# Reading the ids into registers before batch 10 instead of along the way

## The chip, the cores and the metric

The kernel runs on one core of a Trainium2 chip. The metric is the device time of one execution in microseconds (us); lower is better. A core has five engines with a program each: TensorE (PE), VectorE (DVE), ScalarE (ACT), GpSimd (POOL) and SyncE (SP). In front of each engine stands a sequencer, which takes the engine's instructions in their order, keeps registers, and hands work on to the engine.

## The reference

128 batches of a 128 x 512 f32 tile each go through an adapter whose weights are picked by an id of the batch (0 to 9), then a layer norm with gamma and beta of that id, then a residual:

```
w1, w2 = W1[ids], W2[ids]                          # (B,512,128), (B,128,512)
h = relu(einsum('bsh,bha->bsa', x, w1) + b1[ids])
y = x + einsum('bsa,bah->bsh', h, w2) + b2[ids]
n = (y - mean(y)) * rsqrt(var(y) + 1e-5)
out = x + n * gamma[ids] + beta[ids]
```

## The kernel before

W2 and the ten rows of beta, gamma and b2 (spread over all partitions) stay in SBUF for the whole run. Each batch passes through these steps, named in the code: `transpose_x` (PE, L490) and `copy_xT` (ACT, L494) turn x; `down` (PE, L513) multiplies by W1; `relu` (ACT, L521) adds b1; `up` (PE, L535) multiplies by W2 into a PSUM tile `py`, of which there are five; `residual` (DVE, L553) adds x and b2 and sums the rows, after `vector_b2` (DVE, L545) in some batches; `square` (ACT, L576) sums the squares; for a pair of batches `scalar_means` (ACT, L567), `deviation` (ACT, L586) and three small steps `rstd` (DVE, L590, L592, L595) make mean and deviation; `scale` (DVE, L619) multiplies by gamma; `finish` (DVE, L628) adds x plus beta, which `add_beta` (POOL, L507) has made in the tile `o`; `store` (SP, L632) writes a pair of batches. `add_b2` (POOL, L500) makes x plus b2 in one of four tiles `r` for about two thirds of the batches. W1 of a batch comes by a transfer that SP issues or by a copy from SBUF (`stage_w1`, ACT L481, or POOL).

Each of these steps that uses a row of a table needs the batch's id in a register of its own engine. The ids lie in SBUF in two forms: `lang`, one word a batch, and `packed`, 27 words of four ids each for batches 20 to 127 (`NEAR` is 20, `FAR` is 27). A read is a `TENSOR_LOAD` (L271), an instruction of the engine's sequencer. `near` reads four words of `lang` (batches 0-3, 4-7 and so on), `far` four words of `packed` (three at the end), each once an engine; what has been read is kept. So ACT, PE and DVE make five reads of `lang` and seven of `packed` each. `far_at_once` reads all 27 words on POOL. SP reads for its transfers when it comes to them.

The order of instructions on each engine is the order in which the Python code calls the steps (`keep` pins it). The first calls are written out by hand. Then each step is put on a list with a due time in batches (`at`), mostly from the tables `STEPS`, and the list is sorted by due time; the last batches are again written out by hand. So a read whose due time changes moves among the same other steps of its engine, which keep their order.

Of the kernel before, what the change touches and what calls it, by code (L numbers as in the profile page):

```python
# [13 lines left out]
ET = mybir.EngineType  # L14
# [3 lines left out]
G = 4  # L18
# [125 lines left out]
def cond_resid_kernel(ctx: ExitStack, tc: tile.TileContext, x, itok, W1, b1, W2, b2, gamma, beta, out):  # L144
# [18 lines left out]
    def keep(ins):  # L163

        engine = ins.ins.engine
        if engine in last:
            tc.add_manual_dep(ins.ins, last[engine], behind, reason="kept order")
        last[engine] = ins.ins.name
        return ins
# [21 lines left out]
    def xb(b):  # L191
        return xs[b // X][:, b % X, :]
# [62 lines left out]
    NEAR, BITS = 20, 5  # L255
    FAR = (B - NEAR) // 4
# [13 lines left out]
    def read_ids(tile, engine, most, why):  # L270
        loads, vals = nc.values_load_multi_w_load_instructions(  # L271
            tile, engines=[engine], min_val=0, max_val=most, skip_runtime_bounds_check_because=why
        )
        for ins in loads:
            keep(ins)
        return vals

    def near(b, engine):
        g = b // G
        if (g, engine) not in lids:  # L280
            lids[g, engine] = read_ids(
                lang[0:1, g * G : (g + 1) * G], engine, L - 1, "clamped on the chip to 0..L-1 above"
            )
        return lids[g, engine][b % G]
# [13 lines left out]
    def far_at_once(engine):  # L298
        vals = read_ids(packed, engine, ((1 << 4 * BITS) - 1) * H, "four ids of 0..L-1 at five bits each, times H")
        for i in range(0, FAR, G):  # L300
            lids[(NEAR + i) // G, engine] = vals[i : i + G]
# [8 lines left out]
    def lid_h(b, engine):  # L310

        if b < NEAR:
            return near(b, engine) * H
        k, v = far(b, engine)
        if k:
            v = v >> (BITS * k)
        v = v & (((1 << BITS) - 1) * H)
        return v.with_bounds(min_val=0, max_val=(L - 1) * H, guaranteed_mod_val=0, out_of_modulus=H)
# [67 lines left out]
    def spread(r, copier):  # L386
        t = (beta_b, gamma_b, b2_b)[r // L]
        row = p_y.tile([P, H], FP, tag="y", name=f"row_{r}")
        pick_r = pick[:, r : r + 1].to_broadcast([96, P])
        keep(nc.tensor.matmul(row, lhsT=pick_r, rhs=parts[:96, :], start=True, stop=True))  # L390
        dst = t[:, r % L * H : (r % L + 1) * H]
        if copier is nc.scalar:
            keep(nc.scalar.copy(dst, row))
        else:
            keep(nc.vector.tensor_copy(dst, row))
# [21 lines left out]
    def of(parts, b):  # L417
        if b < len(parts[0]):
            return parts[0][b]
        return parts[1][b % steady] if b < closing else parts[2][b - closing]  # L420
# [4 lines left out]
    def turn(b):  # L425
        return of(TURNS, b)
# [4 lines left out]
    def seeded(b):  # L431
        return kind(b) in SEEDED

    def b2_on_gpsimd(b):
        return kind(b) in ON_GPSIMD

    def b2_by_vector(b):
        return kind(b) == "D"
# [63 lines left out]
    def add_beta(b):  # L502
        g, j = divmod(b, 2)
        if g not in os:
            os[g] = op.tile([P, 2, H], FP, tag="o", name=f"o_{g}")
        v = lid_h(b, ET.Pool)
        keep(nc.gpsimd.tensor_tensor(os[g][:, j, :], xb(b), beta_b[:, bass.ds(v, H)], ALU.add))  # L507
# [283 lines left out]
    spread(18, nc.scalar)  # L791
    spread(19, nc.scalar)
    far_at_once(ET.Pool)
    add_beta(0)
    add_beta(1)
    spread(20, nc.scalar)
# [13 lines left out]
    def at(when, step, *args):  # L810
        plan.append((when, len(plan), step, args))

    def when(name, b):
        return b + of(STEPS[name], b)

    for b in range(B):
        if b >= 20 and b % X == 0:
            at(b + X_STEPS[b // X - 10], load_x, b // X)
        if b >= 3:
            for n, engine in ((b + 5, ET.Activation), (b + 5, ET.PE), (b + 6, ET.Pool)):  # L820
                if n < NEAR:
                    at(b + 0.99, lid, n, engine)
        if turn(b) in "Fw":
            at(when("load", b), load_rows if turn(b) == "F" else load_late, b)
        if turn(b) == "F":
            at(when("load", b), load_blocks, b)
            at(when("turn", b), turn_blocks, b)
        elif 5 <= b <= E - 2:
            at(when("transpose", b), transpose_x, b)
            at(when("copy", b), copy_xT, b)  # L830
        if 4 <= b <= E - 3:
            if b2_on_gpsimd(b):
                at(when("r", b), add_b2, b)
            at(when("beta", b), add_beta, b)
            at(when("down", b), down, b)
            at(when("relu", b), relu, b)
        if seeded(b):
            at(when("seed", b), seed, b)
        if FIRST <= b <= E - 1 and turn(b) not in "Fw":
            at(when("w1", b), stage_w1, b)  # L840
        if 2 <= b <= E - 4:
            at(when("up", b), up, b)
# [4 lines left out]
    def at_pair(g, key, step, *args):  # L847
        if g < E // 2 - 3 or (step, *args) in begun:
            at(key, step, *args)

    for g in range(E // 2 - 1):
        b = 2 * g
        for n in (b, b + 1):
            if b2_by_vector(n):
                at_pair(g, when("vb2", n), vector_b2, n)
            at_pair(g, when("stat", n), residual, n)
            at_pair(g, when("square", n), square, n)
        at_pair(g, when("means", b), scalar_means, g)
        at_pair(g, when("root", b), deviation, g)
        for n in (1, 2, 3):  # L860
            at_pair(g, when(f"n{n}", b), rstd, g, n)
        for n in (b, b + 1):
            at_pair(g, when("scale", n), scale, n)
            at_pair(g, when("end", n), finish, n)
        if b % G == 0 and b + G < NEAR:
            at_pair(g, when("scale", b) + 0.001, lid, b + G, ET.DVE)
        at_pair(g, when("store", b), store, g)

    for n in range(0, FAR, G):
        for engine, first in ((ET.Activation, 6.5), (ET.PE, 6.3), (ET.DVE, 7.0)):  # L870
            at(first + n / 2, far, NEAR + n, engine)

    for _, _, step, args in sorted(plan, key=lambda step: step[:2]):
        step(*args)
# [185 lines left out]
```

## Time and profile before

| | |
|---|---|
| time, median of 3 runs (lowest, highest) | 301.47 us (300.65, 301.47) |
| the profiled execution | 300.83 us |
| its span, first to last instruction | 299.1 us |
| busy of the span: PE, DVE, ACT, POOL | 290.8, 288.9, 273.4, 276.3 us |
| granted clock of TensorE | 0.996 |

The profiled execution is a run of its own, 0.64 us below the median; 1.73 us of it lie outside the span. A sequencer's instructions, the reads among them, are not counted as busy; they show as rows of the queues PEldq, ACTq, DVEq, POOLq and SPq. In the rows of groups and lines the numbers of buffers are left out.

### The profile page before, as it was taken

The numbers are of one execution on the slowest core, as the hardware profiler recorded it, in microseconds if no ns is written. First come the engines' busy times: TensorE is split into PE (matmuls) and PEld (weight loads), VectorE is DVE, ScalarE is ACT, GpSimd is POOL, SyncE is SP. The second block draws the span as 40 slices with busy tenths as digits, with TensorE's granted clock in tenths as the row PEclk, the third lists the DMA queues.
The fourth block names the chain that finished last, engine by engine and source line by source line (L and its number), as shares of the span: only waits on it lengthen the run. The fifth ranks groups of instructions, "written<-read, shape, count | busy, mean of one in ns | idle before, by whom it ended". The sixth has DMA issues, their size and how long they took to land. (4 is left out here: it accounts for less than half of the span.)

```text
span 299.1 us, 8487 instructions
## 1 busy us (share of the span) xinstructions
PE 290.8 (97%) x1779; PEld 216.3 (72%) x1779; DVE 288.9 (97%) x780; ACT 273.4 (91%) x760; POOL 276.3 (92%) x238
## 2 busy tenths in 40 slices
PE   7999998999999999999999999999999999999992
PEld 3868776777777777777777777777777777777760
DVE  6999998999999999999999999999999999999995
ACT  4877886999999999999999999999999999899992
POOL 1199998998999999999999999999999999999982
PEclk9999999999999999999999999999999999999998
DMA  6999999989487997869995997859976898993816
GB/s 228 384 388 369 343 312 407 360 287 286 168 279 245 312 390 229 317 206 345 323 301 179 276 403 249 323 191 328 346 226 253 277 355 265 307 346 121 272 50 234
DMA packets 62260, 85.82 MB, mean 287 GB/s; under 512 B 4185, under 2 KB 26212, under 8 KB 62210
## 3 DMA queue, kind: packets, MB, share of 16 engines
q1 hardware_dynamic: 62150, 85.23, 83.8%
q8 instruction: 16, 0.26, 0.4%
q14 instruction: 34, 0.28, 0.3%
q10 hardware_dynamic: 60, 0.05, 0.1%
HBM read 51.71 MB, written 33.55 MB: 285 GB/s over the span
## 5 line engine op out<-in xcount | busy, mean ns | idle before, releaser
L507 POOL TENSOR_TENSOR o<-x,beta_b 128x512 f32<-128x512 f32 x121 | 153.6, 1304 | 12.6 <-DVE beta_b L408 12.6
L513 PEld LDWEIGHTS ph<-xT,w1s 128*128 128x128 f32 x1024 | 126.9, 192 | 15.1 <-ACT hT L521 9.1
L513 PE MATMUL ph<-xT,w1s 128*128 128x128 f32 x1024 | 135.7, 275 | 1.2 <-ACT sq L576 1.1
L500 POOL TENSOR_TENSOR r<-x,b_b 128x512 f32<-128x512 f32 x83 | 106.7, 1305 | 2.9 <-DVE part L592 2.2
L535 PE MATMUL py<-w,hT 128*128 x196 | 100.5, 595 | 0.0
L490 PEld LDWEIGHTS pxT<-ident,x 128*128 128x128 f32 x464 | 60.2, 151 | 52.5 <-issue 38.0
L619 DVE SCALAR_TENSOR_TENSOR py<-py,nmean,gamma_b 128x512 f32<-128x512 f32 x124 | 92.5, 751 | 0.3
L576 ACT ACTIVATE sq<-py,sum 128x512 f32<-128x512 f32 x124 | 86.1, 694 | 2.8 <-DVE py L553 1.0
L628 DVE SCALAR_TENSOR_TENSOR o<-py,rstd,o 128x512 f32<-128x512 f32 x116 | 84.9, 746 | 2.7 <-issue 1.5
L494 ACT COPY xT<-pxT 128x512 f32<-128x512 f32 x116 | 68.3, 588 | 7.9 <-PE pxT L490 6.5
L490 PE MATMUL pxT<-ident,x 128*128 128x128 f32 x464 | 71.3, 277 | 0.1
L553 DVE SCALAR_TENSOR_TENSOR py<-py,r 128x512 f32<-128x512 f32 x88 | 60.7, 690 | 0.0
L521 ACT ACTIVATE hT<-ph,b1T 128x128 f32<-128x128 f32 x128 | 47.7, 373 | 4.8 <-PE ph L513 2.4
L481 ACT COPY w1s<-w 128x512 f32 x80 | 48.7, 622 | 0.2
L535 PEld LDWEIGHTS py<-w,hT 128*128 128x128 f32 x196 | 30.1, 192 | 1.8 <-issue 1.1
L527 PE MATMUL py<-w,hT 128*128 x60 | 30.8, 595 | 0.0
L576 ACT ACTIVATION_READ_ACCUMULATOR sq<-py,sum 128x1 f32 x124 | 25.9, 209 | 0.0
L553 DVE SCALAR_TENSOR_TENSOR py<-py,b_b 128x512 f32<-128x512 f32 x30 | 20.6, 687 | 0.0
L473 ACT COPY py<-x 128x512 f32<-128x512 f32 x30 | 18.0, 599 | 0.2 <-DVE o L628 0.2
L586 ACT ACTIVATE root<-ssq,eps 128x2 f32<-128x2 f32 x62 | 16.9, 273 | 0.5
L567 ACT ACTIVATE nmean<-sum 128x2 f32<-128x2 f32 x61 | 13.0, 213 | 0.3 <-DVE rstd L595 0.2
L553 DVE DVE_READ_ACCUMULATOR py<-py,r 128x1 f32 x88 | 12.3, 139 | 0.0
(83 smaller groups left out, 152.9 us busy)
## 6 DMA issues: line engine op xcount, KB each, us to landing
x<-in_x_dram SPq DMA_DIRECT2D x64, 512.0 KB, 7.3
out_dram<-o SPq DMA_DIRECT2D x62, 512.0 KB, 6.7
w1s<-in_L_cond_W_dram SPq DMA_DIRECT2D x25, 256.0 KB, 7.3
w1s<-in_L_cond_W_dram SPq DMA_DIRECT2D x48, 64.0 KB, 4.1
x<-in_x_dram SPq DMA_DIRECT2D x48, 64.0 KB, 2.0
w<-in_L_cond_W_dram SPq DMA_DIRECT2D x4, 640.0 KB, 8.1
w<-in_L_cond_W_dram SPq DMA_DIRECT2D x1, 1792.0 KB, 9.9
w<-in_L_cond_W_dram SPq DMA_DIRECT2D x1, 768.0 KB, 5.3
```

The source lines that it names most:

```text
L481: keep(nc.gpsimd.tensor_copy(dst, src) if gpsimd else nc.scalar.copy(dst, src))
L490: keep(nc.tensor.transpose(pxs[b][:, k, :], cols, ident))
L494: keep(nc.scalar.copy(xT[b], pxs.pop(b)))
L500: keep(nc.gpsimd.tensor_tensor(rs[b], xb(b), b2_b[:, bass.ds(v, H)], ALU.add))
L507: keep(nc.gpsimd.tensor_tensor(os[g][:, j, :], xb(b), beta_b[:, bass.ds(v, H)], ALU.add))
L513: nc.tensor.matmul(phs[b], lhsT=w1s[b][:, k, :], rhs=xT_of(b, k), start=(k == 0), stop=(k == KC - 1))
L521: keep(nc.scalar.activation(hT[b], phs.pop(b), AF.Relu, bias=b1T[:, bass.ds(lid(b, ET.Activation), 1)]))
L535: keep(nc.tensor.matmul(ys[b], lhsT=hT[b], rhs=w2[:, bass.ds(v, H)], start=not m, stop=True))
L553: nc.vector.scalar_tensor_tensor(ys[b], ys[b], 1.0, r, ALU.mult, ALU.add, accum_out=sum_of(b))
L576: nc.scalar.activation(sq, ys[b], AF.Square, bias=col(sums, b), scale=-float(H), accum_out=col(ssqs, b))
L619: nc.vector.scalar_tensor_tensor(ys[b], ys[b], col(nmeans, b), gamma_b[:, bass.ds(v, H)], ALU.add, ALU.mult)
L628: nc.vector.scalar_tensor_tensor(o, ys[b], rstds[g][:, j : j + 1], o, ALU.mult, ALU.add)
```

## The change

On POOL all five reads of `lang` are made in the opening, right behind the read of `packed`. On ACT, PE and DVE the reads of `lang` for batches 4 to 19 and all seven reads of `packed` are put on one list, one every 0.55 batch from due time 3.9, 3.7 and 4.1 on; the last is due at 9.2 to 9.6. Before, the reads of `lang` were due up to batch 15 and those of `packed` from batch 6.3 to 7.0 on, one every two batches, the last due at 18.3 to 19.0. SP's reads stay. Nothing else is called at another due time.

```diff
     far_at_once(ET.Pool)
+    for n in range(0, NEAR, G):
+        near(n, ET.Pool)
     add_beta(0)
...
-        if b >= 3:
-            for n, engine in ((b + 5, ET.Activation), (b + 5, ET.PE), (b + 6, ET.Pool)):
-                if n < NEAR:
-                    at(b + 0.99, lid, n, engine)
...
-        if b % G == 0 and b + G < NEAR:
-            at_pair(g, when("scale", b) + 0.001, lid, b + G, ET.DVE)
...
-    for n in range(0, FAR, G):
-        for engine, first in ((ET.Activation, 6.5), (ET.PE, 6.3), (ET.DVE, 7.0)):
-            at(first + n / 2, far, NEAR + n, engine)
+    reads = [(near, n) for n in range(0, NEAR, G)] + [(far, NEAR + n) for n in range(0, FAR, G)]
+    for n, (read, b) in enumerate(reads[1:]):
+        for engine, first in ((ET.Activation, 3.9), (ET.PE, 3.7), (ET.DVE, 4.1)):
+            at(first + n * 0.55, read, b, engine)
```

On VectorE, where the first pair of batches is normalised (`part`, `rstd`) and its first batch finished (`o`), before:

```order
L553 SCALAR_TENSOR_TENSOR py_496,sum_516<-py_496,x_141 128x512
L590 SCALAR_TENSOR_TENSOR part_562<-ssq_547,root_561 128x2
L619 ISA
L619 SCALAR_TENSOR_TENSOR py_468<-py_468,nmean_557,gamma_b 128x512
L271 TENSOR_LOAD lang
L592 SCALAR_TENSOR_TENSOR part_562<-part_562,root_561 128x2
L595 SCALAR_TENSOR_TENSOR rstd_600<-part_562,root_561 128x2
L628 SCALAR_TENSOR_TENSOR o_430<-py_468,rstd_600,o_430 128x512
```

The same place after (buffers have other numbers):

```order
L553 SCALAR_TENSOR_TENSOR py_523,sum_552<-py_523,x_141 128x512
L271 TENSOR_LOAD lang x2
L590 SCALAR_TENSOR_TENSOR part_634<-ssq_565,root_633 128x2
L619 ISA
L619 SCALAR_TENSOR_TENSOR py_504<-py_504,nmean_611,gamma_b 128x512
L592 SCALAR_TENSOR_TENSOR part_634<-part_634,root_633 128x2
L271 TENSOR_LOAD lang
L595 SCALAR_TENSOR_TENSOR rstd_699<-part_634,root_633 128x2
L271 TENSOR_LOAD packed
L628 SCALAR_TENSOR_TENSOR o_475<-py_504,rstd_699,o_475 128x512
```

Where one read stood there are four: two in a row ahead of the first small step, one ahead of the third, one ahead of the finish.

On VectorE, where batch 14 is scaled (L619 on `py_1028`) and finished, before:

```order
L619 SCALAR_TENSOR_TENSOR py_1028<-py_1028,nmean_1147,gamma_b 128x512
L271 TENSOR_LOAD lang
L595 SCALAR_TENSOR_TENSOR rstd_1229<-part_1161,root_1160 128x2
L553 SCALAR_TENSOR_TENSOR py_1176,sum_1180<-py_1176,r_1095 128x512
L271 TENSOR_LOAD packed
L628 SCALAR_TENSOR_TENSOR o_825<-py_1028,rstd_1229,o_825 128x512
```

After the change both reads are gone from there, and none of this engine stands behind batch 10; the other rows keep their order.

On TensorE, from `down` of batch 4 (L513 on `ph_636`) to that of batch 6, after:

```order
L271 TENSOR_LOAD lang x2
L513 MATMUL ph_636<-xT_515,w1s_150 128x128 x4
L271 TENSOR_LOAD lang
L490 MATMUL pxT_673<-ident,x_163 128x128 x4
L271 TENSOR_LOAD packed
L513 MATMUL ph_715<-xT_622,w1s_161 128x128 x4
L271 TENSOR_LOAD packed
L535 ISA
L535 MATMUL py_730<-w_92,hT_661 128x512
L490 MATMUL pxT_743<-ident,x_163 128x128 x4
L271 TENSOR_LOAD packed
L513 MATMUL ph_770<-xT_711,w1s_165 128x128 x4
```

Before, one read of `lang` and one of `packed` stood in this stretch. Here there are six.

## The prediction

> **What bounds the kernel now.** I read the page's busy shares first, then the time by stages, then the reads' own rows, then the timeline where they are slow. In the stage rows below the columns are the stretch, its length, then busy time of PE, PE's weight loads, DVE, ACT and POOL, the granted clock, the share of the transfer engines and GB/s.
>
> ```profile
> PE 290.8 (97%) x1779; PEld 216.3 (72%) x1779; DVE 288.9 (97%) x780; ACT 273.4 (91%) x760; POOL 276.3 (92%) x238
> 20.30:49.00 28.70, 28.55 (x181) 22.25 (x180) 28.21 (x72) 23.26 (x69) 28.35 (x23) 1.00 1.09 354
> 49.00:53.00 4.00, 2.92 (x18) 1.89 (x17) 2.53 (x8) 2.72 (x8) 3.27 (x3) 1.00 1.05 407
> 53.00:282.00 229.00, 228.90 (x1449) 173.61 (x1447) 227.80 (x603) 223.53 (x630) 227.14 (x191) 1.00 0.84 283
> ```
>
> From 20 to 49 and from 53 to 282 us VectorE is busy 98 to 99.5% of the time; PE shows as much, but its ends are modelled. VectorE's operations have measured ends, so I take it as the bound: what it loses in that stretch reaches the end, and what it is spared does too. The exception is 49 to 53 us, where all engines rest at once. The timeline there:
>
> ```profile
> 49.33 0.60 PE L490 MATMUL pxT<-ident,x 128*128 128x128 f32 x4
> 49.73 1.27 POOL L500 TENSOR_TENSOR r<-x,b_b 128x512 f32<-128x512 f32 x1 [1.09 <-DVE part L592]
> 50.55 0.20 ACT L576 ACTIVATION_READ_ACCUMULATOR sq<-py,sum 128x1 f32 x1
> 50.93 0.14 DVE L553 DVE_READ_ACCUMULATOR py<-py,r 128x1 f32 x1
> 51.02 1.13 PE L513 MATMUL ph<-xT,w1s 128*128 128x128 f32 x8 [1.08 <-ACT sq L576]
> 52.03 0.59 ACT L494 COPY xT<-pxT 128x512 f32<-128x512 f32 x1 [1.28 <-issue]
> 52.54 0.75 DVE L628 SCALAR_TENSOR_TENSOR o<-py,rstd,o 128x512 f32<-128x512 f32 x1 [1.47 <-issue]
> ```
>
> Idle times stand in brackets: 1.47 us on VectorE, 1.28 on ScalarE, 1.08 on TensorE. ScalarE and VectorE wait for nothing the profile can name. The reads of ids explain it. These are their rows from 18 to 42 us, then from 43 to 60 (duration in ns as minimum/median/maximum, then first and last start):
>
> ```profile
> L271 PEldq TENSOR_LOAD <-packed x5: 329/330/333, 22.1 to 39.5; - x5
> L271 ACTq TENSOR_LOAD <-packed x5: 305/310/310, 23.3 to 39.4; - x5
> L271 DVEq TENSOR_LOAD <-packed x5: 338/342/351, 24.4 to 41.1; - x5
> L271 DVEq TENSOR_LOAD <-lang x4: 340/374/598, 18.6 to 40.7; - x4
> L271 PEldq TENSOR_LOAD <-packed x2: 1253/1686/2119, 43.3 to 48.8; - x2
> L271 ACTq TENSOR_LOAD <-packed x2: 997/1631/2265, 44.2 to 49.7; - x2
> L271 DVEq TENSOR_LOAD <-packed x2: 885/1554/2224, 47.7 to 50.2; - x2
> ```
>
> Up to 41.1 us a read takes about 0.33 us; from 43.3 us on 0.89 to 2.27. VectorE's last one starts at 50.2, lasts 2.22, ends at 52.4, and the finish behind it starts at 52.54. A sequencer with a read in hand passes nothing on, and what it had passed on before lasted until 51.07 (50.93 + 0.14). So a read is free as long as the engine has work in hand that lasts longer: by the last reads the cover is 2.22 - 1.47 = 0.75 us on VectorE, 2.27 - 1.28 = 0.99 on ScalarE, 2.12 - 1.08 = 1.04 on TensorE.
>
> What changed between 41 and 43 us? SyncE's queue issues the first store there:
>
> ```profile
> 40.91 0.41 SPq L632 DMA_DIRECT2D out_dram<-o  x1
> L271 SPq TENSOR_LOAD <-packed x2: 295/300/304, 62.5 to 78.0; - x2
> L271 SPq TENSOR_LOAD <-packed x1: 2339/2339/2339, 88.3 to 88.3; - x1
> L271 SPq TENSOR_LOAD <-packed x1: 381/381/381, 155.6 to 155.6; - x1
> ```
>
> The last three rows are SyncE's own reads under stores: 0.3, 2.34 and 0.38 us. My reading is that a read is slow by chance once stores run, and quick while transfers only load, though the share of the transfer engines is 1.09 already before.
>
> **Part by part: what is removed.** The late reads go. Of their idle time 1.47 us counts, VectorE's, since it is the bound. TensorE's and ScalarE's reads that end beside it go as well; otherwise these engines would be late next. TensorE is spared 1.08 us, so VectorE finds its work ready if it gains no more than about that; beyond it TensorE's modelled time leaves the limit open.
>
> **What is added on VectorE.** Eleven reads lie between due times 4.1 and 9.6 where before there were three in these batches. One behind a 0.75 us operation is covered, like the nine quick ones before, around which VectorE rests nowhere longer than 0.5 us. The exposed places are those where short steps stand between reads. The first pair, before:
>
> ```profile
> 22.43 0.70 DVE L553 SCALAR_TENSOR_TENSOR py<-py,x 128x512 f32<-128x512 f32 x1
> 23.04 0.15 DVE L590 SCALAR_TENSOR_TENSOR part<-ssq,root 128x2 f32<-128x2 f32 x1
> 23.11 0.75 DVE L619 SCALAR_TENSOR_TENSOR py<-py,nmean,gamma_b 128x512 f32<-128x512 f32 x1
> 23.77 0.16 DVE L592 SCALAR_TENSOR_TENSOR part<-part,root 128x2 f32<-128x2 f32 x1
> 23.97 0.16 DVE L595 SCALAR_TENSOR_TENSOR rstd<-part,root 128x2 f32<-128x2 f32 x1
> 24.24 0.75 DVE L628 SCALAR_TENSOR_TENSOR o<-py,rstd,o 128x512 f32<-128x512 f32 x1
> ```
>
> The residual (L553) waits for the operation ahead of it, so the sequencer goes on only when it starts, at 22.43. The two reads of `lang` then take 2 x 0.35 us and, I estimate, 0.1 between them: they end at about 23.25 and the register step and the scale follow, to start at about 23.42 instead of 23.11. Cost: 0.3 us. The read ahead of L595 hides under the scale. L595 needs the result of L592, so the read of `packed` behind it starts with L595 and lasts 0.34; the finish could have followed after 24.24 - 23.97 = 0.27, and now comes after about 0.34 + 0.17 of passing on. Cost: 0.24 us. The next double place (batches 2 and 3, one read ahead of L592, one behind) has a 0.7 us operation over each read: nothing, or at most again 0.3. Sum 0.55 us; the bounds are 0 (each covered, as the nine were) and eleven reads fully exposed, 11 x 0.34 = 3.7. I take 0.55, near the lower end, since nine of the eleven have an operation of about 0.7 us running over them. No gain can come of them, as a read does no work for the engine.
>
> **TensorE, ScalarE, GpSimd.** TensorE's ten reads cost 0.33 each against a cover of 1.04. Two in close order before, with the array's rows around them:
>
> ```profile
> L271 PEldq TENSOR_LOAD <-lang x1: 332/332/332, 34.7 to 34.7; - x1
> L271 PEldq TENSOR_LOAD <-packed x1: 330/330/330, 35.2 to 35.2; - x1
> 34.73 1.02 PE L535 MATMUL py<-w,hT 128*128 x2
> 35.59 0.64 PE L490 MATMUL pxT<-ident,x 128*128 128x128 f32 x4
> 36.06 1.06 PE L513 MATMUL ph<-xT,w1s 128*128 128x128 f32 x8
> ```
>
> No idle in the array: 0 for the double read too (0.66 under 1.04); without cover it would be 0.33 a read. ScalarE has 23.26 us of work in the 28.70 from 20.3 to 49, so short hold-ups go into its rests: 0. On GpSimd four reads of `lang` come ahead of the first addition:
>
> ```profile
> L271 POOLq TENSOR_LOAD <-packed x1: 2446/2446/2446, 6.9 to 6.9; - x1
> L271 POOLq TENSOR_LOAD <-lang x1: 330/330/330, 9.5 to 9.5; - x1
> 14.07 4.98 POOL L507 TENSOR_TENSOR o<-x,beta_b 128x512 f32<-128x512 f32 x4 [12.60 <-DVE beta_b L408]
> ```
>
> The last would end at about 9.5 + 5 x 0.43 = 11.6, and the engine waits for VectorE's rows of beta until 14.07: 0. Without that wait they would cost 4 x 0.33 = 1.3 us. SyncE's reads and every transfer keep their places in the queues.
>
> **The sum.** 1.47 - 0.55 = 0.92 us less. The profiled execution took 300.83 us, so 299.91, say 299.9. The median of the runs lies 0.64 above that execution. Should slow reads be what differs from run to run, the runs will gain more than the profile.
>
> **A rule weighed.** VectorE's quick reads have a median of 0.342 us (`packed`). The Trainium skill, "DMA: Bandwidth & Descriptors", section "Latency and other measured facts", gives such a read a floor of about 600 ns; that speaks against crowding them. By it the sum would be close to no gain. The trace differs: even the slowest engine's 0.342 lies well under that floor, so the row decides.
>
> **The rivals.** (1) *Crowded reads are dearer.* If reads side by side wait for each other, take VectorE's slowest early one, 0.598 us: the double read costs 0.3 + 2 x 0.25 = 0.8, the one behind L595 0.24 + 0.25 = 0.49, together 1.3; gain 0.2, time 300.7. For it: 0.598 occurs. Against: the two of TensorE at 34.7 and 35.2 took 0.33 each. Chance 0.06; the floor above would bring it about.
>
> (2) *The stall is given back.* After 53 us the loads that were issued late (share 1.05) may not be there, or GpSimd's four `r` tiles hold VectorE. GpSimd waited 1.09 us for VectorE at 49.73, so it has that much in hand; no engine's row in these stretches names a transfer as what it waited for. Time 300.8. Chance 0.14.
>
> (3) *Slower: TensorE's lead runs out.* Ten reads with 0.1 of passing on, 0.43 each, lie in 5.5 batches, 12 us; before never more than two close together. If its sequencer does not regain its lead between two reads, 1.04 us of cover is gone after two or three, and the other seven cost 0.33 each: 2.3 us, less the 1.08 spared: +1.2, time 302.0, with VectorE waiting for `py`. It decides from the third read on, at `down` of batch 4 to 6. Against: after the 2.12 us read that emptied the array, `down` took 1.13 instead of 1.06, so the lead is rebuilt quickly. Chance 0.08.
>
> (4) *Slower: it is the last read, not the time.* The slowest read of each engine is the one of three words. If its form is slow, it is slow at batch 9.5 too, the 1.47 us stay and 0.55 come on top: 301.4. Against: SyncE's three-word read, at 155.6, took 0.38. Chance 0.05.
>
> (5) *More than forecast.* All eleven are covered and TensorE's limit is no hindrance: 300.83 - 1.47 = 299.4, or less where a run's other late reads cost more. Chance 0.09.
>
> **How the numbers follow.** The forecast case, 299.4 to 300.4, has what is left, 0.58. Low end of the range: case (5) less 0.4, half of the spread of the three runs (0.82): 299.0. High end: case (4), 301.4, which takes in (1), (2) and a forecast at the median's level (301.47 - 0.92 = 300.6); beyond lie case (3) and a little more. About 0.3% (0.9 us) is what a measurement of this kernel tells from no change, and the forecast stands right there. Since the medians compared come from runs up to 0.64 above the profile's, I give five sixths of the forecast case (0.48) and all of (5) to faster: 0.57. Same: the rest of it, (1), and most of (2): 0.28. Slower: (3), (4) and a little of (2): 0.15.
>
> **What would show it.** Right: no read of ACT, PE or DVE over 0.6 us and none after about 36 us; no rest of all engines near 50 us; on VectorE new rests of about 0.3 us before L590 or L619 and 0.24 before L628 near 23 to 25 us, and no others over 0.3; TensorE without idle from 20 to 49. Wrong: reads of 1 us or more before 36 us, rests in TensorE's array behind its reads, or VectorE resting after 50 us for `r`, `py` or x.

## The result, and the profile after

| | before | after |
|---|---|---|
| median of 7 runs (lowest, highest) | 301.01 us (300.54, 301.47) | 299.90 us (299.68, 300.68) |
| the profiled execution, its span | 300.83, 299.1 us | 300.09, 298.3 us |

The ratio is 0.9966 with an interval of [0.9953, 0.9979]: 1.1 us faster. The stage rows after, with columns as before:

```profile
20.30:49.00 28.70, 28.52 (x180) 22.17 (x178) 27.80 (x70) 22.84 (x68) 28.31 (x23) 1.00 1.09 357
49.00:53.00 4.00, 4.00 (x24) 2.94 (x25) 4.00 (x12) 3.97 (x13) 2.62 (x3) 1.00 1.05 406
53.00:282.00 229.00, 228.92 (x1445) 173.32 (x1444) 227.64 (x603) 223.59 (x629) 228.64 (x192) 1.00 0.84 283
```

From 49 to 53 us PE and DVE are busy for all 4.00 us, where they had 2.92 and 2.53. From 20.3 to 49 us VectorE has 27.80 where it had 28.21: the price lies there, and the timeline below gives its size. The reads from 18 to 60 us, all those of `packed` on the three engines:

```profile
L271 PEldq TENSOR_LOAD <-packed x7: 328/333/770, 22.1 to 28.9; - x7
L271 ACTq TENSOR_LOAD <-packed x7: 303/310/753, 22.1 to 29.9; - x7
L271 DVEq TENSOR_LOAD <-packed x7: 335/342/750, 24.4 to 30.4; - x7
```

No read of these three engines is over 0.8 us, but the longest of each engine, 0.75 to 0.77, is twice its median. It is the last one, of three words. VectorE's timeline where reads are exposed, then where it rested before:

```profile
22.46 0.70 DVE L553 SCALAR_TENSOR_TENSOR py<-py,x 128x512 f32<-128x512 f32 x1
23.35 0.16 DVE L590 SCALAR_TENSOR_TENSOR part<-ssq,root 128x2 f32<-128x2 f32 x1
24.36 0.16 DVE L595 SCALAR_TENSOR_TENSOR rstd<-part,root 128x2 f32<-128x2 f32 x1
24.88 0.75 DVE L628 SCALAR_TENSOR_TENSOR o<-py,rstd,o 128x512 f32<-128x512 f32 x1 [0.37 <-DVE rstd L595]
...
50.97 0.69 DVE L553 SCALAR_TENSOR_TENSOR py<-py,r 128x512 f32<-128x512 f32 x1
51.58 0.74 DVE L628 SCALAR_TENSOR_TENSOR o<-py,rstd,o 128x512 f32<-128x512 f32 x1
```

The first small step starts at 23.35 instead of 23.04, the finish at 24.88 instead of 24.24: 0.64 us later. The finish that had waited until 52.54 starts at 51.58: 0.96 us earlier. Between the two places VectorE has won 0.64 + 0.96 = 1.60 us.

### The profile page after: what moved, and what is told of

Its sections match the earlier page's. It is cut to its first block, busy times and chain, and to the rows that moved or that the text cites. A ratio compares the mean times of both kernels' runs of the same rounds, so it can differ in the third digit from the quotient of the medians.

```text
span 298.3 us, 8487 instructions
## 1 busy us (share of the span) xinstructions
PE 290.9 (98%) x1779; PEld 216.5 (73%) x1779; DVE 288.9 (97%) x780; ACT 273.6 (92%) x760; POOL 276.2 (93%) x238
## 5 line engine op out<-in xcount | busy, mean ns | idle before, releaser
L507 POOL TENSOR_TENSOR o<-x,beta_b 128x512 f32<-128x512 f32 x121 | 152.0, 1279 | 12.6 <-DVE beta_b L408 12.6
L513 PEld LDWEIGHTS ph<-xT,w1s 128*128 128x128 f32 x1024 | 127.0, 192 | 13.4 <-ACT hT L521 8.7
L513 PE MATMUL ph<-xT,w1s 128*128 128x128 f32 x1024 | 135.5, 275 | 0.1
L500 POOL TENSOR_TENSOR r<-x,b_b 128x512 f32<-128x512 f32 x83 | 105.0, 1278 | 2.1 <-DVE part L592 1.8
L490 PEld LDWEIGHTS pxT<-ident,x 128*128 128x128 f32 x464 | 60.2, 151 | 52.4 <-issue 38.2
L619 DVE SCALAR_TENSOR_TENSOR py<-py,nmean,gamma_b 128x512 f32<-128x512 f32 x124 | 92.6, 751 | 0.3
```

The costliest lines, as they stand in the source:

```text
L490: keep(nc.tensor.transpose(pxs[b][:, k, :], cols, ident))
L500: keep(nc.gpsimd.tensor_tensor(rs[b], xb(b), b2_b[:, bass.ds(v, H)], ALU.add))
L513: nc.tensor.matmul(phs[b], lhsT=w1s[b][:, k, :], rhs=xT_of(b, k), start=(k == 0), stop=(k == KC - 1))
L619: nc.vector.scalar_tensor_tensor(ys[b], ys[b], col(nmeans, b), gamma_b[:, bass.ds(v, H)], ALU.add, ALU.mult)
```

## Experiments

Ratios are to the kernel before, run on the same chip.

**The last read with four words, all reads at their old places.** The tile is padded by a word.

```diff
-    packed = const.tile([1, FAR], I32, name="packed")
+    padded = const.tile([1, FAR + 1], I32, name="packed")
+    nc.gpsimd.memset(padded[:, FAR:], 0)
+    packed = padded[:, :FAR]
...
-                packed[0:1, i // G * G : min(i // G * G + G, FAR)],
+                padded[0:1, i // G * G : i // G * G + G],
```

> The kernel before, with the tile packed padded to 28 words, so that the last read of each engine takes four words instead of three; all reads stay where they were. Theory A (a read is slow by the traffic of the stores alone): the last reads on PE, ACT and DVE still take 2.1 to 2.3 us near 50 us, VectorE still rests about 1.47 us, time as before, 301.0 us. Theory B (a read of three words is a dear form, which the stores' traffic makes dearer): the last reads take 0.3 to 1.25 us, like the four-word reads at 43 to 49 us; VectorE rests 0.4 us or less there; time 301.0 less 1.1 to 1.47, 299.5 to 299.9 us, with every read at its old place.

299.56 us (10 runs), ratio 0.9958 [0.9945, 0.9971]. The late reads (43 to 60 us) and VectorE near 50 us, in this kernel, where the read is L273, `residual` L555 and the finish L630:

```profile
L273 PEldq TENSOR_LOAD <-packed x2: 813/985/1157, 43.3 to 48.7; - x2
L273 ACTq TENSOR_LOAD <-packed x2: 734/894/1054, 44.1 to 49.6; - x2
L273 DVEq TENSOR_LOAD <-packed x2: 759/770/782, 47.6 to 50.2; - x2
...
50.88 0.14 DVE L555 DVE_READ_ACCUMULATOR py<-py,r 128x1 f32 x1
51.04 0.75 DVE L630 SCALAR_TENSOR_TENSOR o<-py,rstd,o 128x512 f32<-128x512 f32 x1
```

The last reads take 0.73 to 0.81 us where they took 2.1 to 2.3, and VectorE does not rest (50.88 + 0.14 = 51.02). So theory A is out: the stores make a four-word read dearer, but what stopped all engines was the three-word form under stores. This version, with no read moved, gains as much as the change.

**Only the last read moved.** On all three engines it is due at 13.5.

```diff
-            at(first + n / 2, far, NEAR + n, engine)
+            at(first + n / 2 if n < 24 else 13.5, far, NEAR + n, engine)
```

> The kernel before, with only the last read of each engine (three words) moved from due time 18.3-19.0 to 13.3-13.5, ahead of the first store at 40.9 us, behind a long operation. Theory A: these reads take 0.33 us; theory B: about 0.75 us, as in the changed kernel; by both VectorE's rest of 1.47 us goes and nothing is exposed: 301.0 - 1.47 = 299.5 us. If the gain of the change came from the other ten reads, the time stays near 301.0 us.

299.36 us (6 runs), ratio 0.9952 [0.9936, 0.9969]. The three reads, from 38.2 to 39.2 us:

```profile
L271 DVEq TENSOR_LOAD <-packed x1: 752/752/752, 38.4 to 38.4; - x1
L271 ACTq TENSOR_LOAD <-packed x1: 712/712/712, 38.6 to 38.6; - x1
L271 PEldq TENSOR_LOAD <-packed x1: 774/774/774, 39.0 to 39.0; - x1
```

0.75 us ahead of the first store: theory B. Moving one read of each engine, under a long operation, gives the 1.47 us that the forecast put on the rest near 50 us; moving the other ten early was not needed.

**VectorE's part alone, and all but VectorE's.** In the first the list of early reads holds VectorE's alone (shown below); in the second it holds ScalarE's and TensorE's, GpSimd reads early as in the change, and VectorE where it did before.

```diff
-        if b % G == 0 and b + G < NEAR:
-            at_pair(g, when("scale", b) + 0.001, lid, b + G, ET.DVE)
...
-        for engine, first in ((ET.Activation, 6.5), (ET.PE, 6.3), (ET.DVE, 7.0)):
+        for engine, first in ((ET.Activation, 6.5), (ET.PE, 6.3)):
             at(first + n / 2, far, NEAR + n, engine)
+    reads = [(near, n) for n in range(0, NEAR, G)] + [(far, NEAR + n) for n in range(0, FAR, G)]
+    for n, (read, b) in enumerate(reads[1:]):
+        at(4.1 + n * 0.55, read, b, ET.DVE)
```

> The change on VectorE alone; PE, ACT and GpSimd read where they did before. Theory A (VectorE is the bound, and TensorE has work in hand for it): VectorE loses its 1.47 us rest and gains 0.64 us of exposed reads near 23 to 25 us: 300.2 us. Rival (TensorE is as tight as VectorE): TensorE still rests 1.08 us and ScalarE 1.28 us near 50 us, VectorE waits there for py or for ScalarE, little or nothing is gained: 300.8 to 301.3 us.

> The change on ScalarE, TensorE and GpSimd; VectorE reads where it did before. Theory A (VectorE is the bound): its rest of 1.4 us or more near 50 us stays, nothing is gained: 301.0 us. Rival (TensorE sets the pace): its 1.08 us are won: 299.9 us.

301.15 us, ratio 1.0008 [0.9995, 1.0022], and 300.95 us, ratio 1.0005 [0.9991, 1.0019] (12 runs each): neither part gains. With VectorE's part alone, the array's rest, VectorE's longest wait for it, and then with all but VectorE's, VectorE's rest and what the array waits for later:

```profile
51.42 1.13 PE L513 MATMUL ph<-xT,w1s 128*128 128x128 f32 x8 [0.96 <-ACT sq L576]
DVE py L553 <- PE py L535: 0.6, 1, 0.6
```

```profile
52.50 0.75 DVE L628 SCALAR_TENSOR_TENSOR o<-py,rstd,o 128x512 f32<-128x512 f32 x1 [1.24 <-issue]
58.70 1.12 PE L535 MATMUL py<-w,hT 128*128 x2 [0.74 <-DVE o L628]
```

In the first TensorE still rests 0.96 us for its own slow read (2.10 us), and VectorE, without one, waits 0.60 us for `py`. The `up` that it waits for (52.38 us) follows the array's rest directly, so it is TensorE's lateness that reaches VectorE here. In the second VectorE rests 1.24 us, and TensorE, which had lost nothing, waits 0.74 us for a `py` tile to be finished. VectorE's last operation of the kernel starts at 295.17 and 295.33 us in these two runs, before at 295.37, after the whole change at 294.38. (The second profile is of one of the longer executions, 301.71 us; what it has more lies behind that last operation.) VectorE's part alone also carries the exposed reads near 23 to 25 us, so about 1 us is what it could have gained, and 0.2 is what it gained. Neither engine's rest can go alone; the time falls when both go.

**No stores before 53 us.** The first six pairs of batches are not written, so the time is not to be compared.

```diff
-        at_pair(g, when("store", b), store, g)
+        if g >= 6:
+            at_pair(g, when("store", b), store, g)
```

> The kernel before without the stores of the first six pairs of batches (those rows of the output are not written), so that the first store is issued after 53 us; reads at their old places. If stores under way make the reads slow: the four-word reads of 43 to 49 us take 0.3 to 0.4 us instead of 0.8 to 1.25, the three-word reads near 50 us 0.7 to 0.8 instead of 2.1 to 2.3, and VectorE has no rest over 0.3 us there. If it is the loads, or the time: they stay at 0.8 to 2.3 us and VectorE rests over 1 us.

The reads from 43 to 53 us:

```profile
L271 PEldq TENSOR_LOAD <-packed x2: 332/552/772, 43.6 to 49.0; - x2
L271 ACTq TENSOR_LOAD <-packed x2: 306/509/712, 44.5 to 50.0; - x2
L271 DVEq TENSOR_LOAD <-packed x2: 345/548/750, 47.9 to 50.1; - x2
L271 DVEq TENSOR_LOAD <-lang x1: 345/345/345, 49.5 to 49.5; - x1
```

Each minimum is a four-word read (0.31 to 0.35), each maximum a three-word read (0.71 to 0.77), all as quick as at 30 us. What the transfer engines did meanwhile (columns as before):

```profile
43.00:49.00 6.00, 5.99 (x40) 4.58 (x39) 5.93 (x14) 4.97 (x15) 5.66 (x5) 1.00 1.05 386
49.00:53.00 4.00, 4.00 (x28) 3.04 (x27) 4.00 (x12) 3.97 (x12) 2.98 (x3) 1.00 0.19 71
```

For the four-word reads the comparison is clean: up to 49 us the transfer engines are as busy as before (1.05 in both), now with loads alone, and the reads are quick. From 49 us on the loads run dry as well (0.19, before 1.05), so the three-word reads there show only that it is not the time of the run. That loads alone do not slow this form is shown by the experiment in which only the last read moved: its three-word reads at 38 to 39 us took 0.71 to 0.77 us at a share of 1.13 (36 to 40 us).

**Reads of other sizes on GpSimd.** The words of `lang` and `packed` are read in pieces.

```diff
-    far_at_once(ET.Pool)
-    for n in range(0, NEAR, G):
-        near(n, ET.Pool)
+    for lo, hi in ((0, 3), (3, 7), (7, 8), (8, 10), (10, 16), (16, 20)):
+        read_pool(lang, lo, hi, 0, L - 1)
...
+    for lo, hi in ((0, 4), (4, 7), (7, 8), (8, 12), (12, 15), (15, 16), (16, 20), (20, 23), (23, 24), (24, 27)):
+        at(18.0 + lo, read_pool, packed, lo, hi, NEAR, ((1 << 4 * BITS) - 1) * H)
```

> The changed kernel with GpSimd's reads split in other sizes: in its opening wait 3, 4, 1, 2, 6 and 4 words of lang, and the 27 words of packed as 4, 3, 1, 4, 3, 1, 4, 3, 1, 3 words at due times 18 to 42, when stores run. If the price goes by the word: 0.08 us a word, 3 words 0.25 us. If three words are read singly (the 0.75 us of the three engines' last reads): 1 word about 0.25, 2 words 0.5, 3 words 0.75, 4 words 0.32, 6 words 0.8 us in the opening; under stores the three-word reads cost about 2 to 3 times as much as the four-word reads of the same stretch, and one word about as much as four. It is a look at durations, not at the time of the kernel.

In the opening the pieces of 3 and 4 words, and those of 1 and 2, then those of 4 and 6; below them, under stores, pieces of 4, 3, 4 and 3 words:

```profile
L271 POOLq TENSOR_LOAD <-lang x2: 949/959/969, 3.1 to 4.1; - x2
L271 POOLq TENSOR_LOAD <-lang x2: 299/408/518, 5.1 to 5.5; - x2
L271 POOLq TENSOR_LOAD <-lang x2: 336/859/1382, 6.0 to 7.5; - x2
L271 POOLq TENSOR_LOAD <-packed x1: 1280/1280/1280, 42.7 to 42.7; - x1
L271 POOLq TENSOR_LOAD <-packed x1: 2082/2082/2082, 54.2 to 54.2; - x1
L271 POOLq TENSOR_LOAD <-packed x1: 319/319/319, 63.2 to 63.2; - x1
L271 POOLq TENSOR_LOAD <-packed x1: 812/812/812, 74.1 to 74.1; - x1
```

One word takes 0.30 us, two 0.52, six 1.38 (from word 10 on): 0.22 more for each. Four words from word 16 on take 0.34, but four from word 3 on 0.97, which is 0.30 + 3 x 0.22. So these four words go in one piece when they start at a multiple of four, and otherwise singly; that, I had not expected. A longer read from word 0 is not read singly throughout either: the 27 words of `packed`, which GpSimd reads at once in the other kernels, take 2.45 us, where 0.30 + 26 x 0.22 would be 6.0. The piece of three took 0.95; it is the engine's first read, and first reads cost more (VectorE's took 0.60, the others' 0.49 to 0.53). Under stores each form varies between its quiet price and about three to four times that; single words took 0.29 to 0.91 us there, so these are slowed too. The expectation missed that the start of the piece decides.

**VectorE's reads spaced.** In the changed kernel VectorE's eleven get due times of their own.

```diff
-        for engine, first in ((ET.Activation, 3.9), (ET.PE, 3.7), (ET.DVE, 4.1)):
+        for engine, first in ((ET.Activation, 3.9), (ET.PE, 3.7)):
             at(first + n * 0.55, read, b, engine)
+        at((5.44, 6.2, 6.9, 7.6, 8.3, 9.0, 9.7, 10.4, 11.1, 11.8, 13.5)[n], read, b, ET.DVE)
```

> The changed kernel with VectorE's eleven reads due at 5.44, 6.2, 6.9 and so on every 0.7 up to 11.8, the last at 13.5: still ahead of the first store, but each under an operation of about 0.7 us. If the exposed reads near 23 to 25 us cost the changed kernel 0.64 us: no rest of VectorE over 0.15 us from 21 to 282 us apart from those of before, and 0.998 of the changed kernel's time, 0.995 of the time before, as with the last read alone moved. If these rests are given back elsewhere: 0.9966 as the changed kernel.

299.27 us (5 runs), ratio 0.9941 [0.9928, 0.9954]: the lowest here, clear of the kernel before and 0.6 us under the changed one by the medians, but not clear of the version with the last read alone moved. The place of the exposed reads:

```profile
22.30 0.70 DVE L553 SCALAR_TENSOR_TENSOR py<-py,x 128x512 f32<-128x512 f32 x1
24.11 0.75 DVE L628 SCALAR_TENSOR_TENSOR o<-py,rstd,o 128x512 f32<-128x512 f32 x1
```

From the residual to the finish it is 1.81 us, as before (24.24 - 22.43); in the changed kernel 2.42. The 0.61 us of difference is the price of the reads at the two exposed places.

**The changed kernel with 28 words.** The padding of the first experiment on top of the change.

> The changed kernel with packed padded to 28 words, the last read of each engine four words. The three-word reads took 0.75 us at 29 to 31 us and no engine rested for them, so the time is that of the changed kernel, 0.9966 of before, while the last reads take 0.33 us. If they did cost something, as 0.75 us on TensorE: up to 0.2 us less.

299.88 us (6 runs), ratio 0.9963 [0.9950, 0.9976], as the changed kernel. The last reads of PE and of DVE, from 28.9 to 30.9 us, take 0.33 and 0.37 us:

```profile
L273 DVEq TENSOR_LOAD <-packed x2: 344/358/373, 29.9 to 30.6; - x2
L273 PEldq TENSOR_LOAD <-packed x1: 327/327/327, 29.1 to 29.1; - x1
```

Where they lie under work and ahead of the stores, three words cost nothing more than four. Nor does the padding gain anything by itself here, as by moving the tiles behind it in SBUF; so its gain in the first experiment is that of the late reads.

## Why the prediction was right, and where it was not

- *What is removed.* Forecast: VectorE's 1.47 us, with the other engines' rests going along. It went; by the starts of VectorE's operations it was 1.60 us. That the others had to go along is shown: each part alone gains nothing clear of noise. "VectorE is the bound" was too narrow; TensorE holds the time as well, which its modelled ends (28.55 of 28.70 us) could not tell. The sum held since TensorE's 1.08 us was more than the net gain; how much more TensorE would allow the forecast left open, and with the last read alone moved the gain was 1.46 us.
- *What is added on VectorE.* Forecast 0.55 us at two places, 0.3 and 0.24. Measured 0.61 to 0.64 at those two, and nothing at the other double place. The spaced version confirms it.
- *TensorE, ScalarE, GpSimd at nothing.* The array has no rest there that the page names, its lead held under ten reads, which came within 10 us (19.7 to 29.7), and GpSimd still waits for beta in the opening. Rival (3) did not come.
- *The sum.* Forecast 0.92 us less. VectorE's finish near 52 us came 0.96 earlier, the difference of 1.60 and 0.64; both terms were forecast about 0.1 too low, which cancels. The profiled execution took 0.74 us less (300.83 to 300.09), the medians 1.11. Between VectorE's last operation (0.99 us earlier) and the span's end 0.2 us was given back. The sum did not hold this stretch, in which the last stores land; that their landing is the cause is likely, not shown.
- *Why the reads were slow.* Here the step failed. I had put it down to the stores' traffic and given "it is the last read, not the time" 0.05, on the ground that SyncE's three-word read was the quick one at 155.6 us. That was a misreading: SyncE reads a group when a batch first asks for it, and batch 44, word 24 of 27, is its third to ask, so its three-word read is the one of 2.34 us at 88.3. (With 28 words in the first experiment the same read took 1.07 us.) Rival (4) was half right: the form is dear by itself (0.75), and stores make it 2.1 to 2.3. The forecast survived by luck: the change moves that read ahead of the stores as well, where 0.75 us is covered. For the same reason "no read over 0.6 us" was wrong.
- *Crowded reads are dearer* (rival 1): no. VectorE's two reads in a row, at 22.5 and 22.9 us, took 0.37 and 0.34 us. The 0.598 us that the rival went by is this engine's first read (18.6 us), which takes 0.59 to 0.60 in every run.

What stays open: by which path stores slow a read, and why they slow some reads and not others, was not tried. Whether ScalarE's slow read alone would hold the others was not tried either.

## What to carry to other kernels

A read of registers stops only its own sequencer, so it is free while the engine has longer work in hand, and costs its rest where short dependent steps follow it; put each under a long operation. Look at the longest read apart from the median, and ask what is different about it, its size and where it starts as much as when it runs; padding a table by one word gained here as much as moving some thirty reads. Where two engines hold the time, a rest taken from one of them alone gains little or nothing.

## What the runs showed of the hardware

- With no stores under way, four words that start at a multiple of four took 0.30 to 0.39 us. One, two and three words, four from word 3 and six from word 10 went word by word: 0.30 us for the first and 0.22 for each further one. 27 words from word 0 took 2.45 us, far below that sum. An engine's first read took about 0.2 us more.
- Once stores ran, the same reads took anything from the quiet price up to 1.28 us for four words, and for three up to 2.3 us on the engines that compute and 3.6 on SyncE (at 86.8 us in the run with the last read alone moved). Without stores, at the same time of the run, four words took 0.31 to 0.35 us beside loads that filled the transfer engines.
